# Softmax sums as four 128x32 products at the end of the projection place, with k projected after the output products

## The chip, the cores and the metric

The kernel runs on one core of a Trainium2 chip. The metric is the device time of one execution in microseconds (us); lower is better. Times are compared as medians of several runs, and one further execution is profiled.

## What is computed

The input x is 4 samples of 256 channels by 48x48 = 2304 positions. Four layers are applied in turn, each as `x = x + layer(groupnorm(x))`. What the change touches is the attention, in layer 0 above all:

```python
# layer 0, on the group-normalised x; 8 heads of 64 rows
q, k, v = split(einsum('oc,bchw->bohw', w_qkv, x))
q, k = l2norm over positions of q, k
sim = einsum('bhdi,bhdj->bhij', q, k) * 10.0
attn = softmax(sim)                       # over the 2304 keys j
out = einsum('bhij,bhdj->bhid', attn, v)
x = x + w_out @ out + b_out
# layer 1: a gate from pooled, depthwise-convolved x     layer 3: gate, 3x3 depthwise, norm
# layer 2: single-head attention of the same form (64 rows), then a 1x1 product and batch norm
```

Softmax is computed as exp without a maximum; the output of a block is divided at the end by the sum of the exps over all keys. That sum over keys is what the change recomputes in another shape.

## The kernel before

**Units, slots and places.** The attention is cut into units of 384 queries: 96 in layer 0 (4 samples, 4 pairs of heads, 6 chunks) and 12 in layer 2. A unit has 18 blocks of 128 keys, taken two at a time: 9 groups, one per *slot*. `attend` (from L479) writes the order of all engines by hand, slot by slot; no scheduler moves anything after that, and each engine takes its instructions in the order written. In a slot TensorE gets the `scores` of two key blocks (L309; ScalarE then takes their exp, L315), then what the tables `fills` and `due` hold for that slot, then the products with v of the group before (`weigh`, L329). Scores and value products are 64x64 tiles, four at a time side by side. `add_up` (L349, L355) sums the exp tiles of a unit into `acc`, 128 key rows by 2 heads by 384 queries, on VectorE, with some pairs first added on GpSimd (L340).

Jobs in `fills` carry a rank and run in the order of rank within their slot (5 if none is given). After the ranks in `EVICTED` one waiting "tap" of layer 1, a ScalarE instruction (L876), is put in.

**The projection place.** In slot 2 of every unit (`AT_AFTER` is 11, 11 mod 9 is 2) stand the products that use all 128 rows of the array. `chunk` projects the next pair's q, v and k for 384 positions: q at rank 1 (L604, ScalarE evicts it with a bias, L620), v at rank 2 (L635, ScalarE copies it, L640), and at rank 3 `end`: k (L604), its eviction (L620), the two squared sums of q and k (L626), and the fetch of later input. `out_proj` multiplies the finished unit's output with w_out in two halves of 128 channels (L687); VectorE adds each to x (L700). Its first half has rank 2.5 for samples 1 to 3 and rank 0 for sample 0, its second half rank 4. So the order on TensorE is q, v, first output product, k, second output product; in sample 0 it is first output product, q, v, k, second output product. The results take turns in two PSUM banks (`pj`, two buffers): each product takes the bank of the product two before it, and waits until that one has been evicted.

**The group norms' small products.** A group norm is `squares` and `inverse`, each with a product of 2 columns with `gmat` (L228, L238), in two consecutive places at rank 3.5. They write columns 448 and 449 of k's bank.

**The sums.** A unit's last products stand in slot 0 of the next unit; `last` then files `total` for slot 3 (`AT_TOTAL`), `fold` for slot 2, `invert` for slot 5, `divide` for slot 9, and the output products for slot 11. `total` (L362) makes four 64x64 products of 384 columns with ones, two heads by two halves of the key rows, into two `pj` buffers; ScalarE copies both (128x384, L371) and four DMAs (L375) spread one row of each half over 128 partitions by 6 columns. `invert` adds the two halves, takes the reciprocal and sends it back by DMA for `divide`. There are 104 such totals: 95 in layer 0 and 9 in layer 2. The remaining 4 units use `total_here` and are not touched.

For 89 of the 95 totals of layer 0 the place one slot earlier has a `chunk` in it. In the last 6 it has layer 2's projections instead (L1058, L1079).

Of the kernel before, what the change touches and what calls it, by code (L numbers as in the profile page):

```python
# [14 lines left out]
P = 128  # L15
HW = 48
N = HW * HW
NK = 2
# [60 lines left out]
def usual_path(  # L79
# [86 lines left out]
    )  # L166
    ones = cpool.tile([P, D], F32, name="ones")
    nc.gpsimd.memset(ones, 1.0)

    nb1 = cpool.tile([P, NK], F32, name="nb1")  # L170

# [25 lines left out]
    def gn(b, res, halves=range(NK), slices=range(NSL), first=False, placed=False):  # L197

        if "st" not in res:
            res["st"] = small.tile([P, NK, NSL, 6], F32, tag="gn_st", name="gn_st")  # L200
        st = res["st"]
        if first:
            ps = sc_tile()
            for s in slices:
                for k in halves:
                    rehearse(ps, X[b][:, k, s * SL : (s + 1) * SL])
                    nc.vector.bn_stats(st[:, k, s, :], X[b][:, k, s * SL : (s + 1) * SL])
        for s in () if first else slices:
            for k in halves:
                nc.vector.bn_stats(st[:, k, s, :], X[b][:, k, s * SL : (s + 1) * SL])  # L210
            if s % 2 or len(halves) == NK:
                yield 0
        mv = res.get("mv")
        if mv is None:
            mv = small.tile([P, NK, 2], F32, tag="gn_mv", name="gn_mv")
        for k in range(NK):
            nc.vector.bn_aggr(mv[:, k, :], st[:, k].rearrange("p s f -> p (s f)"))
        gm = small.tile([P, NK], F32, tag="gn_gm", name="gn_gm")

        def columns():  # L220

            if of_k.get("t") == clock["t"]:
                return of_k["ps"][:, 448 : 448 + NK]
            return pj_tile()

        def squares():
            ps = columns()
            nc.tensor.matmul(ps[:, 0:NK], lhsT=gmat, rhs=mv[:, :, 0], start=True, stop=True)  # L228
            nc.vector.tensor_copy(gm, ps[:, 0:NK])
            dev = small.tile([P, NK], F32, tag="gn_dev", name="gn_dev")  # L230
            nc.vector.tensor_sub(dev, mv[:, :, 0], gm)
            res["sq"] = sq = small.tile([P, NK], F32, tag="gn_sq", name="gn_sq")
            nc.vector.tensor_mul(sq, dev, dev)
            nc.vector.tensor_add(sq, sq, mv[:, :, 1])

        def inverse():
            ps = columns()
            nc.tensor.matmul(ps[:, 0:NK], lhsT=gmat, rhs=res["sq"], start=True, stop=True)  # L238
            gv = small.tile([P, NK], F32, tag="gn_gv", name="gn_gv")
            nc.vector.tensor_scalar(gv, ps[:, 0:NK], GN_EPS, None, ALU.add)  # L240
            res["rs_"] = small.tile([P, NK], F32, tag="gn_rs", name="gn_rs", bufs=6)
            rsqrt(res["rs_"], gv)

        def done():
            rs = res["rs_"]
            nm = small.tile([P, NK], F32, tag="gn_nm", name="gn_nm", bufs=6)
            nc.vector.tensor_scalar(nm, gm, -1.0, None, ALU.mult)
            nb = small.tile([P, NK], F32, tag="gn_nb", name="gn_nb", bufs=6)
            nc.vector.tensor_mul(nb, nm, rs)
            res["rs"], res["nb"], res["nm"] = rs, nb, nm  # L250

        if placed:

            t = clock["t"] + 1
            t += (AT_AFTER - t) % NG
            fills.setdefault(t, []).append((3.5, squares))
            fills.setdefault(t + NG, []).append((3.5, inverse))
            due.setdefault(t + NG + 3, []).append(done)
            yield 1
            return  # L260
        yield 3
        squares()
        if first:
            for _ in range(2):
                rehearse(ps, X[b][:, 0, :])
        yield 2
        inverse()
        if first:
            for _ in range(4):
                rehearse(ps, X[b][:, 0, :])  # L270
        yield 2
        done()
        yield 1
# [60 lines left out]
    def add_up(u, g):  # L334
# [19 lines left out]
        for term in ready:  # L354
            nc.vector.tensor_add(u["acc"], u["acc"], term)  # L355

    def total(u):

        ab = [pj_tile()[:, :SL] for _ in range(2)]
        for h, c in enumerate(HALVES):  # L360
            for r, out in zip(HALVES, ab):
                nc.tensor.matmul(  # L362
                    out[c], lhsT=ones[r], rhs=u["acc"][r, h, :], start=True, stop=True
                )
        if "shift" in u["of"]:
            rows = [op.tile([P, SL + 1], F32, tag="o", name="row")[:, :SL] for _ in ab]
        else:
            row = hpool.tile([P, 2, SL], F32, tag="half", name="row")
            rows = [row[:, i, :] for i in range(2)]
        for i in range(2):  # L370
            nc.scalar.copy(rows[i], ab[i])  # L371
        u["l6"] = small.tile([P, 2, LW], F32, tag="l6", name="l6")
        for c in HALVES:
            for i in range(2):
                nc.sync.dma_start(  # L375
                    u["l6"][c, i, :],
                    rows[i][c.start : c.start + 1, :].rearrange("o (p w) -> o p w", w=LW),
                )

    def invert(u):  # L380
        l6, ls = u["l6"], small.tile([P, 2, LW], F32, tag="ls", name="ls")
        nc.vector.tensor_add(ls[:, 0, :], l6[:, 0, :], l6[:, 1, :])
        nc.vector.reciprocal(ls[:, 1, :], ls[:, 0, :])
        u["rinv"] = rpool.tile([P, SL], F32, tag="rinv", name="rinv")
        for c in HALVES:
            r0 = c.start
            nc.sync.dma_start(
                u["rinv"][r0 : r0 + 1, :].rearrange("o (p w) -> o p w", w=LW), ls[c, 1, :]
            )
        for c in HALVES:  # L390
            r0 = c.start
            nc.sync.dma_start(
                u["rinv"][r0 + 1 : r0 + D, :],
                u["rinv"][r0 : r0 + 1, :].unsqueeze(1).to_broadcast([1, D - 1, SL]),
            )
        nc.vector.tensor_add(lsum, lsum, ls[:, 0, :])
        nc.vector.tensor_tensor(lmin, lmin, ls[:, 0, :], ALU.min)

    def take(u):

# [43 lines left out]
        del taps_due[:n]  # L444

    FREE = 10**6
    EVICTED = (1, 2, 3, 4)
    AT_TOTAL, AT_FOLD, AT_INVERT, AT_DIVIDE, AT_AFTER = 3, 2, 5, 9, 11

    def last(u, t):  # L450

        take(u)
        if u.get("soon"):
            todo = [
                (fills, 1, lambda: total_here(u)), (due, 2, lambda: divide(u, nc.vector)),
            ]
            if u.get("final"):
                noted.append(lambda: note(u))
            else:
                todo.insert(1, (due, 2, lambda: fold(u, nc.vector)))  # L460
                todo.append((due, 2, lambda: note(u)))
            after = 3
        else:
            todo = [
                (fills, AT_TOTAL, lambda: total(u)), (due, AT_FOLD, lambda: fold(u, nc.gpsimd)),
                (due, AT_INVERT, lambda: invert(u)),
                (due, AT_DIVIDE, lambda: divide(u, nc.gpsimd)),
            ]
            after = AT_AFTER
# [75 lines left out]
    def project(b, norm, pair):  # L545
# [50 lines left out]
        def qk(s, t):  # L596
# [11 lines left out]
            if s == 0 and direct:  # L608
                for k in range(NK):
                    nc.tensor.matmul(  # L610
                        ps[:, SL : SL + 1], lhsT=at["w"][:, k, t, :],
                        rhs=norm["nm"][:, k : k + 1], start=k == 0, stop=k == NK - 1,
                    )
            if s == 0:
                nc.scalar.copy(at["bias"][:, t : t + 1], ps[:, SL : SL + 1])
            if direct and t:
# [2 lines left out]
            else:  # L619
                nc.scalar.activation(to, ps[:, :SL], AF.Identity, bias=at["bias"][:, t : t + 1])  # L620

        def squares(s):

            for t in range(2):
                junk = rpool.tile([P, SL], mybir.dt.bfloat16, tag="junk", name="junk")
                nc.scalar.activation(  # L626
                    junk, pair["qk"[t]][:, s * SL : (s + 1) * SL], AF.Square,
                    accum_out=at["ss"][:, t, s : s + 1],
                )

        def values(s):
            ps = pj_tile()
# [10 lines left out]

        def chunk(s):

            def end():
                qk(s, 1)
                squares(s)
                if s + 2 < NCH:
                    fetch(s + 2)  # L650

            return [(1, lambda: qk(s, 0)), (2, lambda: values(s)), (3, end)]

        def scale():
            n2 = small.tile([P, 2], F32, tag="n2", name="n2")
# [6 lines left out]
        def rescale(c0, c1):  # L662
# [8 lines left out]

        return {
            "prefetch": prefetch, "norms": norms, "start": start,
            "chunk": chunk, "qk": qk, "squares": squares, "values": values,
            "scale": [
                scale, lambda: rescale(0, 1), lambda: rescale(1, 3), lambda: rescale(3, 6)
            ],
# [639 lines left out]
    order = [(b, p) for b in range(B) for p in range(NPAIR)]  # L1317
    projs = [project(b, norms0[b], pairs[b][p]) for b, p in order]
    n = NCH * NG
    AT_CHUNK = AT_AFTER % NG  # L1320
    for i, (b, p) in enumerate(order):
        work, others = {}, []
        if i + 1 < len(order):
# [78 lines left out]

    for s in range(NCH):
        for t in range(2):
            projs[0]["qk"](s, t)
        projs[0]["squares"](s)
    for fn in projs[0]["scale"]:
        fn()
    for s in range(NCH):
# [1467 lines left out]
```

## Time and profile before

| what | value |
|---|---|
| time, median of 3 runs | 3520.81 us (3519.45 to 3521.15) |
| the profiled execution's own time | 3522.7 us |
| its span, first to last instruction | 3520.9 us |
| TensorE busy | 3438.4 us (98%) |
| VectorE busy | 2559.1 us (73%) |
| ScalarE busy | 2386.1 us (68%) |
| GpSimd busy | 796.8 us (23%) |
| mean granted TensorE clock | 0.995 |

In the profile PE is TensorE's matrix multiplications and PEld its loads of the stationary tile, which overlap them; DVE is VectorE, ACT ScalarE, POOL GpSimd, SP the engine that issues most DMAs. A float32 product appears as two records, so the four products of `total` are eight records (832 for 104 totals). A record's duration includes the way through the array and overlaps the next record; the time that a product costs is the distance from one start to the next. A row of the timeline is a start, a length, the engine, the line, the operation, the tiles and the number of records merged into it; in square brackets stands how long the engine had been idle before it and who ended that.

### The profile page before, as it was taken

The numbers are of one execution on the slowest core, as the hardware profiler recorded it, in microseconds if no ns is written. First come the engines' busy times: TensorE is split into PE (matmuls) and PEld (weight loads), VectorE is DVE, ScalarE is ACT, GpSimd is POOL, SyncE is SP. The second block draws the span as 40 slices with busy tenths as digits, with TensorE's granted clock in tenths as the row PEclk, the third lists the DMA queues.
The fourth block names the chain that finished last, engine by engine and source line by source line (L and its number), as shares of the span: only waits on it lengthen the run. The fifth ranks groups of instructions, "written<-read, shape, count | busy, mean of one in ns | idle before, by whom it ended". The sixth has DMA issues, their size and how long they took to land. (4 is left out here: it accounts for less than half of the span.)

```text
span 3520.9 us, 88613 instructions
## 1 busy us (share of the span) xinstructions
PE 3438.4 (98%) x37158; PEld 1740.7 (49%) x37158; DVE 2559.1 (73%) x3456; ACT 2386.1 (68%) x3855; POOL 796.8 (23%) x666
## 2 busy tenths in 40 slices
PE   9999999999999999999999999999999999999988
PEld 5554555554444444444444444444444444555533
DVE  3555545467888788687887886878887878657777
ACT  5665666665886796557866976679668755555576
POOL 2333333321111000011110110101010106567432
PEclk9999999999999999999999999999999999999999
DMA  2211111111111111121111111111111110000067
GB/s 89 49 26 22 26 22 26 22 26 22 22 32 22 27 22 26 43 57 21 26 22 27 22 26 18 26 22 26 19 25 15 29 13 4 6 6 8 4 150 226
DMA packets 121897, 116.63 MB, mean 33 GB/s; under 512 B 58848, under 2 KB 112976, under 8 KB 120720
## 3 DMA queue, kind: packets, MB, share of 16 engines
q1 hardware_dynamic: 120240, 108.97, 16.4%
q8 instruction: 293, 4.80, 0.6%
q10 hardware_dynamic: 1248, 1.91, 0.2%
q14 instruction: 116, 0.95, 0.1%
HBM read 56.99 MB, written 11.80 MB: 20 GB/s over the span
## 5 line engine op out<-in xcount | busy, mean ns | idle before, releaser
L315 ACT ACTIVATE pt<-sc 128x768 f32<-128x768 f32 x1944 | 1474.8, 811 | 729.6 <-PE sc L309 722.0
L355 DVE TENSOR_TENSOR acc<-acc,pt 128x768 f32<-128x768 f32 x1368 | 1368.1, 1000 | 171.6 <-ACT pt L315 72.1
L329 PE MATMUL av<-pt,v 64*64 64x384 f32 x13824 | 1274.8, 484 | 0.0
L309 PE MATMUL sc<-q,k 64*64 64x384 f32 x13824 | 1270.0, 482 | 0.5 <-ACT pt L315 0.5
L309 PEld LDWEIGHTS sc<-q,k 64*64 64x64 f32 x13824 | 525.5, 133 | 589.4 <-issue 542.7
L329 PEld LDWEIGHTS av<-pt,v 64*64 64x64 f32 x13824 | 518.2, 133 | 599.1 <-issue 565.7
L410 POOL TENSOR_TENSOR o<-o,rinv 128x384 f32<-128x384 f32 x95 | 115.3, 1213 | 1731.2 <-DMA rinv<-rinv 1724.2
L340 POOL TENSOR_TENSOR half<-pt 128x768 f32<-128x768 f32 x189 | 363.0, 1924 | 532.2 <-ACT pt L315 492.5
L700 DVE SCALAR_TENSOR_TENSOR x<-pj,bo,x 128x384 f32<-128x384 f32 x192 | 118.5, 617 | 313.1 <-PE pj L687 311.7
L355 DVE TENSOR_TENSOR acc<-acc,half 128x768 f32<-128x768 f32 x171 | 192.2, 1124 | 207.4 <-POOL half L340 206.4
L876 ACT ACTIVATE prod<-pd,wt 128x256 f32<-128x256 f32 x486 | 337.3, 765 | 0.2
L604 PE MATMUL pj<-xs,w 128*128 128x384 f32 (+1 forms) x720 | 275.4, 505 | 0.0
L604 PEld LDWEIGHTS pj<-xs,w 128*128 128x128 f32 x720 | 124.1, 189 | 127.9 <-issue 38.3
L329 PE MATMUL av<-pt,qv 64*64 64x384 f32 x1728 | 174.7, 492 | 0.0
L309 PE MATMUL sc<-qv,kd 64*64 64x384 f32 x1728 | 171.6, 486 | 2.4 <-ACT pt L315 2.4
L899 DVE TENSOR_REDUCE prod<-prod 128x256 f32<-128x1280 f32 x114 | 168.7, 1480 | 0.7 <-ACT prod L876 0.7
L687 PE MATMUL pj<-o,wo 128*128 128x384 f32 (+1 forms) x384 | 160.1, 500 | 7.2 <-issue 3.6
L635 PEld LDWEIGHTS pj<-w,xs 128*128 128x128 f32 x1080 | 134.5, 191 | 24.2 <-issue 1.2
L349 DVE TENSOR_TENSOR acc<-pt 128x768 f32<-128x768 f32 x99 | 115.5, 1166 | 40.2 <-ACT pt L315 40.2
L406 POOL TENSOR_TENSOR o<-raw 128x384 f32<-128x384 f32 x95 | 128.9, 1357 | 50.5 <-ACT raw L402 50.0
L635 PE MATMUL pj<-w,xs 128*128 128x128 f32 x1080 | 134.9, 275 | 0.0
L402 ACT COPY raw<-av 128x768 f32<-128x768 f32 x108 | 86.3, 799 | 48.3 <-PE av L329 44.9
(291 smaller groups left out, 2421.2 us busy)
## 6 DMA issues: line engine op xcount, KB each, us to landing
xs<-in_x_dram SPq DMA_DIRECT2D x90, 384.0 KB
sh<-pad SPq DMA_DIRECT2D x126, 162.2 KB
rinv<-rinv SPq DMA_DIRECT2D x208, 94.5 KB
out_dram<-x SPq DMA_DIRECT2D x23, 384.0 KB
l<-row SPq DMA_DIRECT2D x416, 1.5 KB
w<-in_wqkv_dram SPq DMA_DIRECT2D x32, 192.0 KB
x<-in_x_dram SPq DMA_DIRECT2D x4, 1152.0 KB
x<-in_x_dram SPq DMA_DIRECT2D x9, 384.0 KB
```

Of the source, the lines that this page charges most:

```text
L309: nc.tensor.matmul(ps[c * D : (c + 1) * D, h, :SL], lhsT=u["of"]["k"][r, j0 : j0 + D], rhs=u["of"]["q"][r, u["qc"]], start=True, stop=True,)
L315: nc.scalar.activation(pt, ps[:, :, :SL], AF.Exp, scale=u["scale"])
L329: nc.tensor.matmul(u["av"][h * D : (h + 1) * D, half, :SL], lhsT=value(u, j, h)[r], rhs=pt[r, h, :], start=j == 0, stop=j == JB - 1,)
L340: nc.gpsimd.tensor_add(half, pts[0], pts[1])
L355: nc.vector.tensor_add(u["acc"], u["acc"], term)
L406: eng.tensor_add(u["sum"], u["raw"][:, 0, :], u["raw"][:, 1, :])
L604: nc.tensor.matmul(ps[:, :n], lhsT=at["w"][:, k, t, :], rhs=xs[s][:, k, :n], start=k == 0, stop=k == NK - 1,)
L635: nc.tensor.matmul(ps[:, i * P : (i + 1) * P], lhsT=xs[s][:, k, i * P : (i + 1) * P], rhs=at["w"][:, k, 2, :], start=k == 0, stop=k == NK - 1,
L687: nc.tensor.matmul(ps[:, :n], lhsT=wo[:, p, k * P : (k + 1) * P], rhs=o["o"][:, :n], start=True, stop=True,)
L700: nc.vector.scalar_tensor_tensor(xs, ps[:, :SL], pair["bo"][:, k : k + 1], xs, ALU.add, ALU.add)
L876: nc.scalar.activation(bufs[n % 3][:, :, min(n, 1) + i].rearrange("p (r c) -> p r c", c=AS), pd[:, PAD + dr : PAD + dr + AS, PAD + dc : PA ...
L899: nc.vector.tensor_reduce(to, bufs[n % 3][:, :, : min(n, 1) + len(taps)], AX.X, ALU.add)
```

## The change

Three things move together.

1. `total` becomes eight products of 96 columns in 128x32 tiles. A new constant `step1` (128x48, ones in columns 16 to 31) gives a stationary tile of 32 columns with ones in the first 16 (e = 0) or the last 16 (e = 1). Tile j holds one head and two quarters of the queries, so the whole sum over 128 key rows lies in 128x96 numbers, complete, with no halves to add. In a place with a `chunk` it is written into columns 392 to 487 of k's bank, otherwise into a `pj` buffer. One copy (128x96) and one DMA follow, in place of two copies (128x384) and four DMAs, and `invert` loses its addition.
2. `total` moves from slot 3 to slot 2 of the same unit (in layer 2, units with a "shift", it stays in slot 3), at rank 4.6. k's product moves from rank 3 to rank 4.5, behind both output products; its eviction and its square are separate jobs at rank 4.7; the square of q moves to rank 2.2.
3. The norms' small products get jobs of their own (`of_means`, `of_squares`, rank 4.65), ahead of k's eviction, with VectorE's part at rank 4.8, and write columns 500 and 501.

The order on TensorE in a place with a chunk becomes: q, v, first output product, second output product, k, total, small product (sample 0: first output product, q, v, second output product, k, total, small product).

```diff
+    step1 = cpool.tile([P, 48], F32, name="step1")
+    nc.gpsimd.memset(step1, 0.0)
+    nc.gpsimd.memset(step1[:, 16:32], 1.0)
...
             if of_k.get("t") == clock["t"]:
-                return of_k["ps"][:, 448 : 448 + NK]
+                return of_k["ps"][:, 500 : 500 + NK]
...
-            fills.setdefault(t, []).append((3.5, squares))
-            fills.setdefault(t + NG, []).append((3.5, inverse))
+            fills.setdefault(t, []).extend([(4.65, of_means), (4.8, squares)])
+            fills.setdefault(t + NG, []).extend([(4.65, of_squares), (4.8, inverse)])
...
     def total(u):
-        ab = [pj_tile()[:, :SL] for _ in range(2)]
-        for h, c in enumerate(HALVES):
-            for r, out in zip(HALVES, ab):
+        if of_k.get("t") == clock["t"]:
+            ps = of_k["ps"][:, 392 : 392 + QC]
+        else:
+            ps = pj_tile()[:, :QC]
+        for e in range(2):
+            for j in range(4):
+                h, q = j // 2, 2 * (j % 2) + e
                 nc.tensor.matmul(
-                    out[c], lhsT=ones[r], rhs=u["acc"][r, h, :], start=True, stop=True
+                    ps[32 * j : 32 * j + 32], lhsT=step1[:, 16 - 16 * e : 48 - 16 * e],
+                    rhs=u["acc"][:, h, q * QC : (q + 1) * QC], start=e == 0, stop=e == 1,
                 )
...
-        for i in range(2):
-            nc.scalar.copy(rows[i], ab[i])
-        u["l6"] = small.tile([P, 2, LW], F32, tag="l6", name="l6")
-        for c in HALVES:
-            for i in range(2):
-                nc.sync.dma_start(
-                    u["l6"][c, i, :],
-                    rows[i][c.start : c.start + 1, :].rearrange("o (p w) -> o p w", w=LW),
-                )
+        row = small.tile([P, QC], F32, tag="row", name="row")
+        nc.scalar.copy(row, ps)
+        u["l"] = small.tile([P, LW], F32, tag="l", name="l")
+        nc.sync.dma_start(u["l"], row[0 : P : 16, :].rearrange("g (p w) -> g p w", w=LW))
...
-    EVICTED = (1, 2, 3, 4)
+    EVICTED = (1, 2, 4, 4.7)
...
-                (fills, AT_TOTAL, lambda: total(u)), (due, AT_FOLD, lambda: fold(u, nc.gpsimd)),
+                (fills, at_total, (4.6, lambda: total(u))), (due, AT_FOLD, lambda: fold(u, nc.gpsimd)),
...
             def end():
-                qk(s, 1)
-                squares(s)
+                at["evict"]()
+                square(s, 1)
                 if s + 2 < NCH:
                     fetch(s + 2)
-            return [(1, lambda: qk(s, 0)), (2, lambda: values(s)), (3, end)]
+            return [
+                (1, query), (2, lambda: values(s)), (2.2, lambda: square(s, 0)), (4.5, key),
+                (4.7, end),
+            ]
```

## The prediction

> **What bounds the kernel now.** I read the page's busy lines first, then who waited for whom on PE and PEld, then the timeline of PE through some places. TensorE is the bound:
>
> ```profile
> PE 3438.4 (98%) x37158; PEld 1740.7 (49%) x37158; DVE 2559.1 (73%) x3456; ACT 2386.1 (68%) x3855; POOL 796.8 (23%) x666
> ```
>
> So only what changes PE's own sequence counts, and that is best seen start to start. This is PE around one place of sample 1 (columns: start, length, engine, line, operation, tiles, records):
>
> ```profile
> 1322.05 1.47 PE L309 MATMUL sc<-q,k 64*64 64x384 f32 x16
> 1323.45 1.56 PE L604 MATMUL pj<-xs,w 128*128 128x384 f32 x4
> 1324.85 1.50 PE L635 MATMUL pj<-w,xs 128*128 128x128 f32 x12
> 1326.18 0.81 PE L687 MATMUL pj<-o,wo 128*128 128x384 f32 x2
> 1326.91 1.56 PE L604 MATMUL pj<-xs,w 128*128 128x384 f32 x4
> 1328.31 0.81 PE L687 MATMUL pj<-o,wo 128*128 128x384 f32 x2
> 1329.05 1.52 PE L329 MATMUL av<-pt,v 64*64 64x384 f32 x16
> 1330.39 1.47 PE L309 MATMUL sc<-q,k 64*64 64x384 f32 x16
> 1331.68 0.82 PE L362 MATMUL pj<-acc,ones 64*64 64x384 f32 x8
> 1332.32 1.47 PE L329 MATMUL av<-pt,v 64*64 64x384 f32 x16
> ```
>
> The reader is to see four prices. Sixteen 64x64 records take 1.29 us (1330.39 to 1331.68), so a side-by-side group of four takes 0.322 for its 384 columns. The total takes 0.64 and has no gap on either side. Entering the place costs 0.22 (1322.05 to 1323.45 is 1.40 and 1323.45 to 1324.85 is 1.40, each for 1.29 of work); leaving it costs 0.15 (0.74 for 0.645, then 1.34 for 1.29). And k waits: 0.73 for the 0.645 of the output product before it and 1.40 for its own 1.29, together 0.19. What it waits for stands in the list of waits of the weight loads (total us, times, longest):
>
> ```profile
> PEld pj L604 <- ACT v L640: 34.3, 64, 0.5
> ...
> PEld pj L238 <- ACT k L620: 10.7, 8, 1.5
> PEld pj L228 <- ACT k L620: 10.3, 8, 1.3
> ```
>
> k takes v's bank with only one 0.645 us product between; that happens in 64 places. The norms' small products wait for k's eviction in 16.
>
> **The change, part by part.** *Total, 89 places with a chunk.* Out go 0.645 us of PE. In come 16 records in four groups of four. The nearest row for 128x32 tiles is the last layer's convolution between two 64x64 pieces:
>
> ```profile
> 3373.04 0.88 PE L1507 MATMUL w<-y,Ww 64*64 64x384 f32 x8
> 3373.85 2.14 PE L1730 MATMUL cv<-sh,taps 96*32 96x384 f32 x24
> 3375.92 0.88 PE L1507 MATMUL w<-y,Ww 64*64 64x384 f32 x8
> 3376.72 1.50 PE L1730 MATMUL cv<-sh,taps 96*32 96x384 f32 x16
> ```
>
> 24 records take 2.07 us; six groups at 0.322 are 1.93, the other 0.14 is one change of tile shape, and the 64x64 piece has 0.80 for 0.645. So four 32-column tiles do run side by side, and there and back costs about 0.29, one way 0.14. With 96 columns a group is 0.322/4 = 0.081, four are 0.325. Going from k through the total to the value products needs two changes of shape where one stood, so the total costs 0.325 + 0.14 = 0.465, a gain of 0.18 each: 89 x 0.18 = **16.0 gained**. Bounds of the unknown (no row has 96 columns): below, the group cannot be cheaper than its columns; above, a 32-column weight load lasts 0.109, issued when the group before starts, so 0.129 a group with the spread of 0.02 over the four, 0.048 more for three intervals. I take 0.081, because one-column products on 64-column tiles (L1028: eight in the 0.21 us from 2732.12) start far closer than their own weight loads last (0.138).
>
> [...]
>
> *k behind both output products, 64 places (samples 1 to 3).* Banks alternate, so now the second output product takes v's bank and inherits the 0.19 unchanged, and k takes the first output product's bank, which VectorE empties. In the row above that addition runs:
>
> ```profile
> 1327.03 0.62 DVE L700 SCALAR_TENSOR_TENSOR x<-pj,bo,x 128x384 f32<-128x384 f32 x1 [2.27 <-PE pj L687]
> ```
>
> It ends 1327.65; from an evicting instruction's end to useful work on PE passes 0.16 (v's copy ends 1326.86; k's second record shows it began in effect at 1327.02). k could start at 1327.81. The second output product would end at 1327.02 + 0.645 = 1327.66. The new stall is 0.14: 64 x 0.143 = **9.2 lost**. That holds where VectorE is free. Going through the 64 starts of L700 against the ends of L687, it starts later in 20: 10 times by 0.19 (the bias column comes first), 5 times by 0.9 to 2.0 behind the gate's long operations (L1006), 5 times by 0.2 to 0.35, 9.5 us in all. Today a 1.29 us product covers most; the second output product pays 3.6 of it. With half the cover k pays all: **5.9 lost**.
>
> *Sample 0, 24 places.* Its order was first output product, q, v, k, second: no wait, as k took q's bank with v between. Now the second output product takes q's and k takes v's with 0.645 between, the 0.19 of samples 1 to 3: 24 x 0.195 = **4.7 lost**.
>
> *Small products, 16 places.* In a place with one, k's start to the value products is 3.29 (846.00 to 849.29) against 2.14 without (1326.91 to 1329.05): 1.15 each, the wait for k's eviction (0.58) above all. Moved ahead of it, they still stand behind the total's copy in the same bank, and the order of the changed program shows them waiting for ScalarE. The copy: 128x384 takes 0.478, 128x192 takes 0.318 (L1084), so 128x96 about 0.24. From the total's last group: 0.02 and 0.24 to its end, 0.04 to the copy, 0.24 for it, 0.16 back to PE, 0.11 for the first record and 0.23 for the second and the way out, less the 0.24 from that group to the value products without them: 0.80. Gain 0.36 x 16, and twice 0.19 for a bias copy that k's eviction carried: **6.1 gained**. Without the wait it would be 0.3 a place better, at worst (waiting for k's eviction after all) nothing is gained.
>
> *The other 15 totals.* The six beside layer 2's projections: 0.465 and a wait for VectorE of about 0.13, 0.05 better each. The nine of layer 2 stay in slot 3 between 64x64 tiles: two changes, 0.62 against 0.645, 0.03 better each. Two products there (L238 at 2954.26, L1022 at 3036.69) wait 0.77 for the total's copies today, and get a bank of their own. 0.3 + 0.27 + 1.54: **2.1 gained**.
>
> *At nothing.* ScalarE loses two copies (0.87) and gets one of 0.24; its other work in the place is the same, q's square moves into the 0.98 us in which it waited for k, so the exps after the place are not later. `acc` is complete 5 us and more before a place of layer 0 ends, so the total one slot earlier finds it ready; without that it would wait on VectorE's chain. SP issues one DMA for four; the fetch queued behind it serves a place 59 us on. Two memsets of POOL fall before x has landed (PE waits 5.2 for it). `invert` loses an addition VectorE has time for.
>
> Sum: 16.0 + 6.1 + 2.1 - 9.2 - 5.9 - 4.7 = **4.4 gained**. The profiled execution's own 3522.7 (its span of 3520.9 and 1.8 around it) becomes 3518.3; the runs' median lies 1.9 below that execution, so **3516**.
>
> **Rivals.** *Slower: the weight loads bound the groups of four.* Place: inside the total. Price: 0.129 instead of 0.081 in three intervals, 104 x 0.144 = 15, so 3531. It turns the gain over when a group passes 0.096. For it: all groups of 32-column tiles in the trace have 0.322 to hide a load of 0.109. Against: the one-column products. *Faster: k's weights go ahead.* If only the multiplication waited and the weights were loaded under the product before, 0.107 of each new stall falls away, 88 x 0.107 = 9.4: 3507. Against: the waits above are the weight loads'. *It doesn't do what it says:* the small products still end up behind k's eviction; 6.1 not gained, 3522. Against: the copy stands ahead of the eviction in ScalarE's order. *VectorE later than read:* k now waits for it in 64 places, and each 0.1 us of lateness costs 6.4; with 0.15 more it is 3526.
>
> **Chances.** Forecast 0.66 (its own range 3511 to 3522), weight loads 0.10, weights ahead 0.13, not done 0.05, VectorE later 0.06. A measurement can tell about 0.2% (7 us) from no change. Faster by more: weights ahead 0.13 and 0.14 from the forecast's lower end, 0.27. Slower by more: 0.10 and 0.03 of VectorE, 0.13. Within: 0.60. The range 3506 to 3529 leaves out the weight loads' 0.10 and some tails.
>
> **What would show it.** Right: the total's records 0.08 us apart by fours and some 0.33 long behind k; the value products about 0.14 after; in samples 1 to 3 a new entry, k's weight load waiting for VectorE's L700 (its new line) 64 times, and in sample 0 for v's copy 24 times; small products waiting for a copy of about 0.24. Wrong: groups 0.11 or more apart, starts of k right behind the output products, or value products that wait for exps.

## The result and the profile after

The changed kernel takes **3508.51 us**, the median of 8 runs (3503.65 to 3511.34), beside 3520.97 us of the kernel before in 8 runs: a ratio of 0.9964, 95% interval 0.9955 to 0.9973, or 12.5 us less. The forecast was 3516 (4.4 less), with 3511 to 3522 as its own range and 3506 to 3529 as the range stated for the time: the result lies in the second and below the first. To a gain large enough to tell, 7 us or more, the prediction gave a chance of 0.27, to a difference too small to tell 0.60. The sign and the waits that it named came true; the gain is near three times what the sum gave. The profiled execution has a span of 3501.9 us (3503.65 with what lies around it), the shortest of the eight. Line numbers have moved: total is L381 (was L362), its copy L386 (L371), k's and q's product L615 (L604), v's L649 (L635), output products L710 (L687), their addition L723 (L700), small products L231 and L245 (L228, L238), scores L322, value products L342.

The page's busy line:

```profile
PE 3430.2 (98%) x37990; PEld 1728.2 (49%) x37990; DVE 2541.1 (73%) x3352; ACT 2331.2 (67%) x3751; POOL 793.9 (23%) x668
```

TensorE is still the bound. It has 832 records more than before and is busy 8.2 us less. PE through the same place of sample 1 that the prediction showed at 1322.05 (start, length, engine, line, operation, tiles, records):

```profile
1319.79 1.47 PE L322 MATMUL sc<-q,k 64*64 64x384 f32 x16
1321.19 1.56 PE L615 MATMUL pj<-xs,w 128*128 128x384 f32 x4
1322.59 1.50 PE L649 MATMUL pj<-w,xs 128*128 128x128 f32 x12
1323.92 1.65 PE L710 MATMUL pj<-o,wo 128*128 128x384 f32 x4
1325.44 1.56 PE L615 MATMUL pj<-xs,w 128*128 128x384 f32 x4
1326.93 0.54 PE L381 MATMUL pj<-acc,step 128*32 128x96 f32 x16
1327.40 1.52 PE L342 MATMUL av<-pt,v 64*64 64x384 f32 x16
1328.74 1.47 PE L322 MATMUL sc<-q,k 64*64 64x384 f32 x16
```

Read it start to start. The two output products are one row now and take 1.52 for 1.29 of work: 0.19 of the rest is the wait for v's copy that k had before, and 0.04 is the first part of a new wait of k for VectorE. k takes 1.49: its 1.29, the other 0.10 of that wait, and 0.09 for the way into the new tile shape. The total takes 0.47: four groups that add up to 0.33, and 0.14 for the change of shape. Leaving costs 0.05 (1.34 for 1.29), as before.

Who the weight loads waited for (total us, times, longest us):

```profile
PEld pj L710 <- ACT v L654: 34.3, 64, 0.5
...
PEld pj L615 <- DVE x L723: 28.8, 53, 1.6
...
PEld pj L615 <- ACT v L654: 12.8, 24, 0.5
...
PEld pj L231 <- ACT row L386: 4.6, 8, 0.6
PEld pj L245 <- ACT row L386: 4.6, 8, 0.6
```

These are waits of the weight loads; part of each is covered by the product still running, so that 0.54 of wait here (34.3 us over 64) is 0.19 in the products' starts. The first line is k's old wait, inherited by the second output product, 34.3 us to the digit. The second (samples 1 to 3, 53 of the 64 places; the list has the 11 with a bias column under another releaser) and the third (sample 0, 24 times) are the two waits that the new order makes. The last two are the small products, which now wait for the total's copy (0.24 long) instead of k's eviction (0.58).

**Where the time went.** Cut every execution into three: the layer-0 places (start of the first place with a chunk to the start of the last, each from the scores ahead of it), from there to the end of the last attention product (the last pair and layer 2, called the second part below), and the tail. Half-clock stretches are counted in the trace's record of the granted clock: in the second part of before each is 3413 ns, or two together 6827, at a granted 0.50. Half of its length, 1.707 us, is the estimate of what one loses where TensorE works all through it. The column "without them" takes that off the second part for each.

| kernel | places | second part | half-clock stretches in it | second part without them | tail |
|---|---|---|---|---|---|
| before | 2658.59 | 646.14 | 5 | 637.6 | 171.7 |
| before, again (before2) | 2657.07 | 649.62 | 7 | 637.7 | 168.1 |
| changed | 2651.17 | 638.99 | 4 | 632.2 | 167.2 |
| changed, again (after2) | 2651.20 | 639.43 | 4 | 632.6 | 169.5 |
| order alone (only_order) | 2672.04 | 648.84 | 7 | 636.9 | 171.7 |
| small products alone (only_small) | 2642.78 | 651.48 | 9 | 636.1 | 170.8 |
| shape alone (only_shape) | 2654.41 | 644.66 | 6 | 634.4 | 170.6 |
| changed, k first (kfirst) | 2647.79 | 638.78 | 3 | 633.7 | 168.3 |
| changed, small products first (smallfirst) | 2640.99 | 641.08 | 5 | 632.5 | 168.9 |
| both of these (both) | 2638.08 | 645.97 | 7 | 634.0 | 167.3 |
| total in the output product's bank (best) | 2629.73 | 642.18 | 6 | 631.9 | 168.3 |

So the change is worth 5.9 us in the places and 5.3 in the second part, 11.2 together; the rest of any difference between two executions is the number of half-clock stretches and a tail that lies between 167 and 172 us for every kernel and that no edit here touches. The 5.3 is the less certain figure: TensorE stands idle for up to 1.9 us in one pair of these stretches in the kernel before, and counted only where it works, the second part comes to 638.5 and 638.6 before and 632.5 and 633.1 after, a gain of 5.7.

### The profile page after: what moved, and what is told of

Read it like the earlier page. It is cut to its first block, busy times and chain, and to the rows that moved or that the text cites. A ratio compares the mean times of both kernels' runs of the same rounds, so it can differ in the third digit from the quotient of the medians.

```text
span 3501.9 us, 89386 instructions
## 1 busy us (share of the span) xinstructions
PE 3430.2 (98%) x37990; PEld 1728.2 (49%) x37990; DVE 2541.1 (73%) x3352; ACT 2331.2 (67%) x3751; POOL 793.9 (23%) x668
## 4 chain that ended last, share of the span: by engine, by line
PE 86%; DVE 9%; issue 2%; ACT 1%; POOL 1%; DMA 1%; DVEq 0%; SPq 0%; POOLq 0%; ACTq 0%
PE av L342 33%; PE sc L322 33%; PE pj L615 8%; PE pj L710 3%; PE pj L649 3%; DVE acc L368 3%; PE cv L1753 2%; PE pj L381 1%; PE pj L966 1%; PE pj L1081 1%; DVE x L1029 1%; ACT kd L1087 0%; DVE x L1848 0%; DVE x L723 0%; DMA sh<-pad 0%
## 5 line engine op out<-in xcount | busy, mean ns | idle before, releaser
L342 PE MATMUL av<-pt,v 64*64 64x384 f32 x13824 | 1274.7, 484 | 0.0
L322 PE MATMUL sc<-q,k 64*64 64x384 f32 x13824 | 1269.9, 482 | 0.5 <-ACT pt L328 0.5
L322 PEld LDWEIGHTS sc<-q,k 64*64 64x64 f32 x13824 | 525.5, 133 | 589.4 <-issue 558.5
L342 PEld LDWEIGHTS av<-pt,v 64*64 64x64 f32 x13824 | 518.2, 133 | 564.4 <-issue 521.6
L723 DVE SCALAR_TENSOR_TENSOR x<-pj,bo,x 128x384 f32<-128x384 f32 x192 | 118.1, 617 | 256.0 <-PE pj L710 254.7
L615 PE MATMUL pj<-xs,w 128*128 128x384 f32 (+1 forms) x720 | 277.5, 508 | 3.9 <-DVE x L723 3.9
L615 PEld LDWEIGHTS pj<-xs,w 128*128 128x128 f32 x720 | 124.0, 189 | 143.6 <-DVE x L723 28.8
L342 PE MATMUL av<-pt,qv 64*64 64x384 f32 x1728 | 171.9, 494 | 0.0
L322 PE MATMUL sc<-qv,kd 64*64 64x384 f32 x1728 | 167.9, 485 | 2.4 <-ACT pt L328 2.4
L710 PE MATMUL pj<-o,wo 128*128 128x384 f32 (+1 forms) x384 | 159.7, 513 | 5.2 <-issue 3.6
L649 PEld LDWEIGHTS pj<-w,xs 128*128 128x128 f32 x1080 | 134.5, 191 | 24.1 <-issue 1.2
L386 ACT COPY row<-pj 128x96 f32<-128x96 f32 x104 | 24.9, 240 | 179.3 <-PE pj L381 179.3
L362 DVE TENSOR_TENSOR acc<-pt 128x768 f32<-128x768 f32 x99 | 113.5, 1146 | 41.9 <-ACT pt L328 41.9
L415 POOL TENSOR_TENSOR o<-raw 128x384 f32<-128x384 f32 x95 | 120.5, 1269 | 72.7 <-ACT raw L411 72.6
L649 PE MATMUL pj<-w,xs 128*128 128x128 f32 x1080 | 134.9, 275 | 0.0
```

Of the source, the lines that this page charges most:

```text
L322: nc.tensor.matmul(ps[c * D : (c + 1) * D, h, :SL], lhsT=u["of"]["k"][r, j0 : j0 + D], rhs=u["of"]["q"][r, u["qc"]], start=True, stop=True,)
L342: nc.tensor.matmul(u["av"][h * D : (h + 1) * D, half, :SL], lhsT=value(u, j, h)[r], rhs=pt[r, h, :], start=j == 0, stop=j == JB - 1,)
L415: eng.tensor_add(u["sum"], u["raw"][:, 0, :], u["raw"][:, 1, :])
L615: nc.tensor.matmul(ps[:, :n], lhsT=at["w"][:, k, t, :], rhs=xs[s][:, k, :n], start=k == 0, stop=k == NK - 1,)
L649: nc.tensor.matmul(ps[:, i * P : (i + 1) * P], lhsT=xs[s][:, k, i * P : (i + 1) * P], rhs=at["w"][:, k, 2, :], start=k == 0, stop=k == NK - 1,
L710: nc.tensor.matmul(ps[:, :n], lhsT=wo[:, p, k * P : (k + 1) * P], rhs=o["o"][:, :n], start=True, stop=True,)
```

## The experiments

Places are compared one by one between executions: two of the same kernel agree to some thousandths of a us in all but a few. "An ordinary place" holds the q, v, k, output products and total only.

**1. The two kernels again.** No edit. For the changed kernel:

> The changed kernel once more, unaltered, for a second profile: which parts of the difference from the kernel before come back in another execution. In the first profile the layer-0 places account for 7.4 us of the gain, the six places of the last pair for 0.7, layer 2 for 6.4 and the tail (the last 180 us) for 4.4, together 18.9, while the runs' medians differ by 12.5. Theory (the places are the gain, the rest is mostly a good draw of that execution): the layer-0 places again 7.4 within 0.5, layer 2 and the tail together 3 to 7 rather than 10.8, and the total near 3508.5. Rival (layer 2 and the tail are really 10 us shorter by the freed copies and DMAs): both again above 4 us each and a time near 3504.

Measured: 3504.99 us (4 runs, 3502.81 to 3506.44) beside 3520.98: 16.0 below, where the 8 runs above had 12.5. The places repeat to 0.03 us. Layer 2 and the tail differ from the first profile of before by 8.2 us, between the two theories; only the count of half-clock stretches, in the table above, told what of it is the change. For the kernel before:

> The kernel before once more, unaltered, for a second profile. Theory (the work up to 2900 us repeats to the nanosecond, and executions of one kernel differ by how many 3.41 us stretches at half the clock fall into layer 2 and the tail, 1.71 us each): the layer-0 places again 2658.6 within 0.1; the rest from the last place on differs from the first profile's 817.8 by about 1.7 for each stretch more or less. Rival (the spread of executions is spread over the whole kernel): the places differ by over 1 us.

Measured: 3520.87 us in one run. From the last place on it takes 817.70 against 817.80 us, with seven half-clock stretches in the second part and two in the tail against five and three. In the second part each is worth its 1.7 (637.6 and 637.7 without them); in the tail, where TensorE often stands, the count explains only part of the difference. The places differ by 1.52 us, and 1.50 of it is one place, at 2102 us: a miss of "within 0.1", and past the 1 us of the rival, though not spread over the kernel as the rival has it. VectorE's rows in question, of before and then of before2 (the bracket is its idle time and what ended it):

```profile
2089.54 0.17 DVE L382 TENSOR_TENSOR ls<-l 128x6 f32<-128x6 f32 x1 [1.23 <-DMA l<-row]
```

```profile
2088.03 0.16 DVE L382 TENSOR_TENSOR ls<-l 128x6 f32<-128x6 f32 x1
```

In the execution that the prediction was made from, a DMA with the sums landed late once, VectorE stood 1.23 us, its chain ran late into the next place, and the second output product waited 1.5 us there. It is no property of the kernel, and I had read it as one. Gains in the places are therefore taken from before2's 2657.07.

**2. The order alone.** The kernel before with k, its eviction and the small products moved, total as it was.

```diff
-    EVICTED = (1, 2, 3, 4)
+    EVICTED = (1, 2, 4, 4.7)
...
-            return [(1, lambda: qk(s, 0)), (2, lambda: values(s)), (3, end)]
+            return [
+                (1, query), (2, lambda: values(s)), (2.2, lambda: square(s, 0)), (4.5, key),
+                (4.7, end),
+            ]
...
+            fills.setdefault(t, []).extend([(4.75, of_means), (4.8, squares)])
```

> The kernel before with the order alone changed: k behind both output products, its eviction at 4.7 and the small products behind that eviction; the total stays four 64x64 products in slot 3. Theory (putting k behind both output products costs): 0.14 a place in samples 1 to 3, some 0.19 a place in sample 0 and 0.2 to 0.5 where VectorE is late (11 places with a bias column among them), and small products as dear as before or dearer: the 89 places together 12 to 18 us longer than before's, so 3533 to 3539 plus or minus the 4 us by which executions vary. Rival (the order itself is worth something, by ScalarE's earlier square of q and the later eviction): the places within 3 us of before's.

Measured: 3533.06 us (5 runs) beside 3519.31, ratio 1.0034 (1.0020 to 1.0047). Its places are 15.0 us longer. By kind of place: 0.145 in ordinary places of samples 1 to 3, 0.188 in those of sample 0, 0.40 in the 11 with a bias column, 0.63 to 0.71 in five more where VectorE is late; the places with v's bias product get 0.1 to 0.15 cheaper. Putting k last costs what the theory says; it is worth nothing by itself.

**3. The small products alone.** The kernel before with each small product directly behind k, ahead of k's eviction; VectorE's part stays at rank 3.5.

```diff
-            fills.setdefault(t, []).append((3.5, squares))
-            fills.setdefault(t + NG, []).append((3.5, inverse))
+            fills.setdefault(t, []).extend([(3.05, of_means), (3.5, squares)])
+            fills.setdefault(t + NG, []).extend([(3.05, of_squares), (3.5, inverse)])
...
-    EVICTED = (1, 2, 3, 4)
+    EVICTED = (1, 2, 3.1, 4)
...
-            return [(1, lambda: qk(s, 0)), (2, lambda: values(s)), (3, end)]
+            return [
+                (1, query), (2, lambda: values(s)), (3, key), (3.1, end),
+            ]
```

> The kernel before, with its order and its total, and only the norms' small products moved directly behind k's product, ahead of its eviction, so that they wait for nothing. Theory (a small product cost 1.15 us by its wait for k's eviction and costs about 0.2 without any wait): 16 times 0.95, the places 14 to 15.5 us shorter than before's, a time of 3503 to 3509. Rival (what they wait for only turns up behind them, as k's eviction now starts later and the second output product or the value products wait): under 8 us.

Measured: 3509.07 us (4 runs), ratio 0.9964 (0.9948 to 0.9979). The places are 14.3 us shorter, 0.94 in each ordinary place with a small product, and next to nothing turns up behind them (one place loses 0.37). This edit alone brings about as much as the whole change, although its execution had nine half-clock stretches in the second part where the changed kernel had four. Without them it is the larger: 14.3 in the places and 1.5 behind them, against 11.2.

**4. The shape alone.** The kernel before with the new `total` (in a `pj` buffer, one copy, one DMA), left in slot 3.

```diff
+            ps = pj_tile()[:, :QC]
+        for e in range(2):
+            for j in range(4):
+                h, q = j // 2, 2 * (j % 2) + e
                 nc.tensor.matmul(
-                    out[c], lhsT=ones[r], rhs=u["acc"][r, h, :], start=True, stop=True
+                    ps[32 * j : 32 * j + 32], lhsT=step1[:, 16 - 16 * e : 48 - 16 * e],
+                    rhs=u["acc"][:, h, q * QC : (q + 1) * QC], start=e == 0, stop=e == 1,
                 )
...
+            at_total = AT_TOTAL
```

> The kernel before with the total's new shape alone, left where it was in slot 3 between 64x64 tiles and in a pj buffer of its own; one copy of 128x96 and one DMA. Theory (the shape pays only where it replaces a change of tile shape that is there anyway): two changes of shape, 0.33 and 0.28 to 0.30 for the changes, against 0.645 a total, so the layer-0 places and slot 3 together gain 0 to 3 us; whatever else it gains (5 to 8 us) is in layer 2 behind 2900 us, where ScalarE's copies and the buffers that they held are gone; a time of 3512 to 3518. Rival (the cheaper total gains the same 0.18 wherever it stands): 16 us in layer 0 and a time near 3500.

Measured: 3512.74 us (8 runs), ratio 0.9983 (0.9973 to 0.9994). The places gain 2.7 us: 0.017 in nearly all of them, and some 1.2 in a handful where VectorE was late. PE around a total there:

```profile
1329.26 1.47 PE L322 MATMUL sc<-q,k 64*64 64x384 f32 x16
1330.66 0.54 PE L381 MATMUL pj<-acc,step 128*32 128x96 f32 x16
1331.13 1.52 PE L342 MATMUL av<-pt,v 64*64 64x384 f32 x16
1332.47 0.82 PE L322 MATMUL sc<-q,k 64*64 64x384 f32 x8
```

The scores take 1.40 for 1.29 ahead of it and the value products 1.34 behind it. With the 0.47 in between that is 0.628, against 0.645 of the old total. Two changes of tile shape eat the cheaper product. In the place one of them is there anyway: that is why 0.18 of the fewer columns' saving is left there and 0.017 here. The second part, free of half-clock stretches, gains 3.2 us here, less than the 5 to 8 expected. The old total held both `pj` buffers there until two copies, 0.87 us together, were done; that this makes up the 3.2 is not shown, beyond the two waits that the prediction named.

**5. k ahead of the second output product again.**

```diff
-    EVICTED = (1, 2, 4, 4.7)
+    EVICTED = (1, 2, 3.1, 4)
...
-                (1, query), (2, lambda: values(s)), (2.2, lambda: square(s, 0)), (4.5, key),
-                (4.7, end),
+                (1, query), (2, lambda: values(s)), (2.2, lambda: square(s, 0)), (3, key),
+                (3.1, lambda: at["evict"]()), (4.7, end),
```

> The changed kernel with k's product back ahead of the second output product in samples 1 to 3 (rank 3), and its eviction right behind; total stays at the end of the place in k's bank, so that it waits for k's eviction instead of following k at once. Theory (the cheaper shape of the total pays, the new place of k only costs): the stall behind VectorE (0.145 in 64 places) goes back to 0.19 or less on v's copy, which is +0.05 each, but sample 0 loses no wait at 24 places (0.195 there) and the places with a bias column (11 of 0.22) get their cover back; total's wait for k's eviction, about 0.10, is paid in 89 places or hidden by the second output product. In all 4 to 9 us faster than the changed kernel, 3500 to 3504. Rival (having k, total and small products in a row at the end is what pays): 9 to 15 us slower than the changed kernel, 3517 to 3523, by the wait of total and small products for k's eviction.

Measured: 3501.51 us (4 runs) beside 3504.99 of the changed kernel, 3.4 us shorter in the places. The sign and the ordinary place are as expected (0.049 in samples 1 to 3, 0.092 in sample 0, 0.31 with a bias column), the sum falls short of 4: the total now waits for k's eviction, 0.095 where ScalarE is free, some 0.2 more in the places where a bias is copied first (L630) or v's bias product follows, and 0.74 in the one place that has no output products to cover it. The order costs, but the bank of the total has a price too.

**6. The small products ahead of the total.**

```diff
-            fills.setdefault(t, []).extend([(4.65, of_means), (4.8, squares)])
-            fills.setdefault(t + NG, []).extend([(4.65, of_squares), (4.8, inverse)])
+            fills.setdefault(t, []).extend([(4.55, of_means), (4.8, squares)])
+            fills.setdefault(t + NG, []).extend([(4.55, of_squares), (4.8, inverse)])
```

> The changed kernel with the small products of the norms directly behind k and ahead of the total (rank 4.55), so that they wait for no copy. Theory (a small product still costs the 0.43 us in which it waits for the total's copy, 16 of them): 6.5 to 7 us faster than the changed kernel, 3501 to 3503. Rival (that wait is covered elsewhere, or VectorE's reading of the small columns then keeps the total or k's eviction waiting): within 2 us of the changed kernel.

Measured: 3495.81 us (4 runs), ratio to before 0.9927 (0.9910 to 0.9943), 9.2 us below the changed kernel in the same chip's runs and 10.2 in the places: more than the 7 expected. The same place in the changed kernel and then in this one:

```profile
847.32 0.54 PE L381 MATMUL pj<-acc,step 128*32 128x96 f32 x16
848.21 0.38 PE L231 MATMUL pj<-gn_mv,gmat 128*128 128x2 f32 x2 [0.36 <-ACT row L386]
848.53 1.52 PE L342 MATMUL av<-pt,v 64*64 64x384 f32 x16
```

```profile
845.87 0.28 PE L231 MATMUL pj<-gn_mv,gmat 128*128 128x2 f32 x2
846.08 0.54 PE L381 MATMUL pj<-acc,step 128*32 128x96 f32 x16
846.54 1.52 PE L342 MATMUL av<-pt,v 64*64 64x384 f32 x16
```

Total and small product take 1.21 above and 0.67 below. 0.43 of that is the wait for the copy. The other 0.1, and 0.09 more at the end of k, is a change of shape that I had left out: behind the total, the small product goes back from 128x32 to 128x128 tiles before the value products go on to 64x64.

**7. Both, with the total in k's bank.** Experiments 5 and 6 together, the small products at rank 3.05, directly behind k.

```diff
-            fills.setdefault(t, []).extend([(4.65, of_means), (4.8, squares)])
+            fills.setdefault(t, []).extend([(3.05, of_means), (4.8, squares)])
...
-                (4.7, end),
+                (3.1, lambda: at["evict"]()), (4.7, end),
```

> The changed kernel with k back at rank 3 and the small products directly behind k, but with the total left in k's bank at the end of the place: it differs from the best version only in the bank that the total is written to, and from the version with k first only in the small products. Theory (the total's wait for k's eviction costs 0.095 in an ordinary place and more where ScalarE is late; a small product that waits for nothing saves 0.5 to 0.85 in 16 places): the layer-0 places 2637 to 2641 us, 9 shorter than with k first and 7 to 11 longer than in the best version. Rival (the bank of the total does not matter and the best version gains only by the small products): within 3 us of the best version's 2629.7.

Measured: 3497.54 us in one run; places 2638.08, in the middle of the expected 2637 to 2641.

**8. The total in the second output product's bank.** As 7, but `total` writes columns 392 to 487 of that product's bank, directly behind it, and VectorE's addition of it comes at rank 4.65.

```diff
-        if of_k.get("t") == clock["t"]:
-            ps = of_k["ps"][:, 392 : 392 + QC]
+        if of_o.get("t") == clock["t"]:
+            ps = of_o["ps"][:, 392 : 392 + QC]
...
-        return [((2.5 if b else 0, 4)[k], lambda k=k: part(k)) for k in range(NK)]
+        return [
+            (2.5 if b else 0, lambda: part(0)()), (4, second), (4.65, lambda: hold["add"]()),
+        ]
```

> The changed kernel with k back ahead of the second output product, the small products directly behind k (ahead of its eviction), and the total written into columns 392 to 487 of the second output product's bank, directly behind it, with VectorE's addition of that product behind the total. Theory (each order-made wait is avoidable: 0.145 in 64 places, 0.195 in 24, 0.22 more in 11 with a bias column, 0.63 in 16 with a small product): the places 22 to 28 us shorter than the changed kernel's 2651, and with layer 2 as there a time of 3477 to 3484. Rival (the waits come back in another place, as VectorE's addition is 0.35 later and the next unit's products or divisions wait for it, or the small product delays k's eviction into a wait): under 15 us, 3490 or more.

Measured: **3488.08 us** (4 runs, 3486.66 to 3489.69) beside 3519.31, ratio 0.9907 (0.9891 to 0.9924): 31 us below the kernel before, 20 below the changed one's 3508.51 and 17 below its 3504.99 of experiment 1. It is above the 3477 to 3484 that was expected. PE at the end of the place at 1309.38:

```profile
1314.24 1.56 PE L615 MATMUL pj<-xs,w 128*128 128x384 f32 x4
1315.64 0.81 PE L709 MATMUL pj<-o,wo 128*128 128x384 f32 x2
1316.37 0.54 PE L381 MATMUL pj<-acc,step 128*32 128x96 f32 x16
1316.84 1.52 PE L342 MATMUL av<-pt,v 64*64 64x384 f32 x16
```

From k to the value products it is 2.60 us; the changed kernel has 2.75 from its second output product (1324.65, 0.73 behind the first) to them for the same work. The 0.145 is gone, and in sample 0 the 0.19. The places come out 21.4 shorter than the changed kernel's, a little under the 22 expected: in five places 0.26 to 0.8 us comes back, where the second output product waits for a VectorE that is late behind other work, and 1.0 us in each of two where v's bias product (L580) waits for VectorE's addition, which now stands behind ScalarE's copy of the total.

## Why the prediction was right in kind and short in size

Its terms, against the places of before2 and the experiments:

| term of the sum | predicted | measured | from |
|---|---|---|---|
| total in the place, 89 | 16.0 gained | 15.8 | 0.645 to 0.468 in each |
| k's wait for VectorE, 64 places | 9.2 lost | 9.3 | 0.145 in an ordinary place |
| sample 0, 24 places | 4.7 lost | 4.5 | 0.188 in only_order |
| VectorE's lateness | 5.9 lost | 4.3 | what those places lost beyond 0.145 |
| small products, 16 | 6.1 gained | 6.9 | 0.42 in twelve, 0.61 and 0.31 in two each |
| v's bias product, 14 places | not in the sum | 1.3 gained | 0.10 each, behind the total and not an output product |
| **places** | **2.3 gained** | **5.9** | 2657.07 to 2651.17: 5.9 |
| the other 15 totals, and what follows them | 2.1 gained | 5.3 | second part without half-clock stretches |

*The total.* The step from the last layer's convolution holds to 0.003: 0.33 for sixteen records, 0.138 for the change, 0.468 against the predicted 0.465. The rival of the weight loads (0.129 a group) is out: in the total at 1326.93 the groups start 0.106, 0.083 and 0.082 apart.

*k behind the output products.* In the place at 1319.79, VectorE's addition of the first output product:

```profile
1324.77 0.62 DVE L723 SCALAR_TENSOR_TENSOR x<-pj,bo,x 128x384 f32<-128x384 f32 x1 [3.09 <-PE pj L710]
```

It ends at 1325.39. With 0.16 more that makes 1325.55, and k's 1.49 from 1325.44, less the 0.1 of the way into the new shape and its own 1.29, shows the same. The order alone (experiment 2) isolates the price. That k's weights might go ahead is out as well: the wait list names the weight load 53 times, and the stall comes in full.

*The step that failed* was the term of the other 15 totals: it was put at 2.1, most of it from the two products that the trace showed waiting 0.77 for the total's copies, and what lies behind the last place gained 5.3. Only the waits named in the list were counted. The shape alone gives 3.2 there (experiment 4), the small products directly behind k 1.5 (experiment 3), the order 0.8 (experiment 2). These come near 5.3 together (counted only where TensorE works they are 3.9, 1.6 and 1.7, against 5.7), but they are gains of three kernels and not parts of one: the gap of 3.1 us ahead of L943 (below), where TensorE waits for ScalarE's `pd`, is 2.8 with the shape alone, 2.2 with the order alone, 1.7 with the small products alone and 1.8 in the changed kernel. This gap is 0.3 to 1.4 us shorter in them than before, and the busy share of TensorE, 98% before and in the changed kernel, does not show it. Which waits make up the rest of the 5.3 stays open.

*VectorE's lateness* was over-charged by 1.6, but not in the reading of the order: with the order alone (experiment 2) the same places lose 6.4. The single late DMA of the profiled execution is not the reason either, as both the 9.5 and the 3.6 hold it. What was put at nothing is the other half of the change, the addition that `invert` loses and "VectorE has time for". With the new total VectorE is less late: in one place its addition of the first output product starts 0.92 us after that product has ended in before2 (at 1386.02), as in only_order, but 0.34 after it with the shape alone (1385.08), and 0.36 in the changed kernel. Before2, then only_shape:

```profile
1386.94 0.61 DVE L700 SCALAR_TENSOR_TENSOR x<-pj,bo,x 128x384 f32<-128x384 f32 x1
```

```profile
1385.42 0.61 DVE L723 SCALAR_TENSOR_TENSOR x<-pj,bo,x 128x384 f32<-128x384 f32 x1
```

The dropped addition takes 0.16 us; how the chain comes to end 0.6 earlier was not followed.

*The small products* were costed at 0.80 and take 0.74, so the saving of 0.36 became 0.42. The larger miss lies in what a place without the wait was said to be worth, 0.3: moving the small product ahead of the total brought 0.63 (experiment 6), as the wait is 0.43 and the change of shape behind the total was not in the sum.

So the change is a gain of 15.8 for the shape and some 6.9 for the small products, of which its own order takes back 18.1, and 1.3 and 5.3 that were not, or not fully, seen. The order is the wrong part of it: undone, with the small products directly behind k and the total in the second output product's bank, the same products give 31 us (experiment 8).

## What to carry to other kernels

A change of tile shape has a price of its own (0.14 to 0.2 us here), so put a product of another shape where the shape changes anyway, and price it start to start. When a product is moved in a rotation of two banks, ask for each product behind it whose eviction it now waits for; spare columns of a bank that is evicted late can hold a small result almost for nothing (the waits of 0.145 and 0.19 went, and 1.0 us came back in two places). And compare executions place by place: that separates 0.02 us of an edit from 5 us of chance.

## What the runs showed of the hardware

Much of the spread of the runs is the clock's. Of the 18 runs of the kernel before beside experiments 2 to 4 and 8, the six at a mean granted clock of 0.996 took 3515.49 to 3516.89 us and the seven at 0.994 took 3519.17 to 3524.81. Two executions of the same kernel before, around the same gap ahead of layer 1's products (L943 waiting for ScalarE's `pd`), by windows (window, its length, PE busy and records, granted clock, DMA share, GB/s). First the first profile, then before2:

```profile
2980.79:2984.20 3.41, 1.47 (x20) 1.00 0.00 0
2984.20:2987.62 3.42, 2.30 (x42) 1.00 0.00 0
```

```profile
2979.13:2982.55 3.42, 0.54 (x12) 1.00 0.00 0
2982.55:2985.96 3.41, 3.41 (x40) 0.50 0.02 5
```

The gap is 3.1 us in both. In the first execution it is split over two windows, TensorE is busy 1.47 of 3.41 us in the first of them and 2.30 in the second, and nothing follows; in the second nearly all of it falls into one window, and the next 3.41 us run at half the clock. The stretches of one execution lie on one grid (2915.9 and 3049.0 us are 39 steps of 3.41 apart), whose phase differs between executions: here one boundary is at 2980.8 us in the first and at 2982.6 in the second. So the same gap costs 1.65 us or nothing: from L943's first record to the next product pass 2.71 us in the first execution (2985.32 to 2988.03) and 4.36 in the second (2982.01 to 2986.37). How busy TensorE was in one window does not settle it, though: in the first execution the window ahead of 2915.9 us had 1.98 of 3.41 us busy, more than the 1.47 above, and the next one ran at half the clock; so did the one behind the window from 3083.17 us, with 1.40 of 3.41 us busy. What does settle it is not shown.
